# A decoder on one core: the recurrent cell's last steps and the head of causal attention, from generators and a scheduler to one written list of steps

## The chip, the cores and the metric

The program runs on one core of one Trainium2 chip. The metric is the device time of that core in microseconds (us), from the start of the program to its end. The core's engines have one instruction queue each and run beside one another: PE (TensorE: matrix products, and PEld for its weight loads), DVE (VectorE), ACT (ScalarE), POOL (GpSimd) and SP (SyncE, which issues DMAs). An engine works through its queue in order, and an instruction that waits for another engine holds everything behind it on its own.

## The reference, cut to what matters

The reference is a pre-norm decoder of two layers on `x` of 2 x 1024 x 256, all in float32. The change lies where the first layer's recurrent cell ends and the second layer's causal attention begins:

```python
def step(c, xt):
    ft = sigmoid(xt @ wf.T + c @ uf.T + bf)
    it = sigmoid(xt @ wi.T + c @ ui.T + bi)
    gt = tanh(xt @ wc.T + c @ uc.T + bc)
    return ft * c + it * gt, None
c_final, _ = lax.scan(step, c0, x)              # two steps: the leading axis of x is time
h = tanh(einsum('tbi,oi->tbo', x, wo) + c_final @ uo.T + bo)     # both steps' rows
...
qkv = einsum('bsd,hde->bhse', x, Wqkv) + bqkv   # 16 heads of 16, on the normed x
score = where(causal, einsum('bhsd,bhtd->bhst', q, k), -inf)
attn = softmax(score / sqrt(16)); y = attn @ v  ...  out = y @ Wout + bout
```

Both are residual: `x = x + cell(norm(x))`, then `x = x + causal(norm(x))`. Cross attention and a mixture of experts follow and end the program.

## The kernel before, in words

**The cell** (class `Cell`). Rows are held as 16 tiles of 128 rows; the normed x is held transposed (`xT[0]` for the first time step, `xT[1]` for the second). `gates(pool, step, state)` computes a step for two column halves `nb` and two halves `mc` of the features: three gates each, a gate being 2 (first step) or 4 (second step) float32 products of 128x128 by 128x512 into a PSUM tile `ps_t` (L1370), a sigmoid or tanh on ACT (L1378), and three DVE operations that make the new state (L1385 to L1388). `out(pool, t)` adds the cell's output to one of the 16 tiles of x: four products of 128x256 (L1411), a bias add on DVE (L1415), tanh on ACT (L1416), and the add to x on DVE (L1417).

**Causal attention** (class `Causal`). Eight units `u` = batch entry x group of four heads; each head takes 32 of the 128 partitions. `prepare(b)` clears the values (POOL), takes the norm's statistics (DVE, a power on POOL), norms (ACT, L1480), adds an output bias to x on POOL (L224), transposes (PE, L1489; copied by ACT, L1490) and makes the values (PE, L1496; DVE, L1503). `project(u)` makes four halves of keys and queries (PE, L1524; bias on ACT, L1531). `maxima(u)` takes the row maxima that the softmax subtracts, in 24 steps: for one query tile and a pair of heads (`pr` 0 or 1, so half of the 128 partitions) two products of 32 rows by up to 512 columns into one tile `ps_s` (L1565), on the diagonal a causal add on DVE (L1573), and a reduction on DVE (L1581). `augment(u, half)` transposes the maxima and adds them to the queries (L1591, L1593). `attend(u)` has 24 steps too: scores of a pair of heads into two tiles `ps_t` (L1640), exponentials on ACT (L1675), a mask on POOL (L1633), and, two entries late (`LAG`), the product with the values into `ps_o` (L1605).

**PSUM.** Under `banks("ps_e", 2, 4, 0)` there are two `ps_s` and four `ps_t` tiles, under `banks("ps_b", 2, 3, 1)` two, three and one `ps_o`.

**What sets the order.** `cell.scan` (both steps of the cell) is written in program order. The 16 `out` steps, `prepare(0)` and `project(0)` (generator `start`) stand outside a manual schedule, so the framework's scheduler orders them, with four `ps_t`. Then the cell's memory is closed, `Cross` is built (its weights are loaded by SP, L2699 on, and it clears and masks small tiles on POOL, L1857 to L1878), and `causal.run` follows in program order: twelve steps of maxima of unit 0 beside the eight projection halves of units 1 and 2, `augment(0, 0)`, then the loop over units. In the loop's pass for unit 0 each of the first eight steps runs two maxima and each of the other sixteen runs one, so that the maxima come to stand 20 steps ahead of the attention (`LEAD`):

```python
        for i in range(n - self.LEAD + 8):
            max_step()
            next(side, None)
        self.augment(0, 0)
        ...
                max_step()
                if u == 0 and i < 8:
                    max_step()
                next(attend, None)
```

From unit 1 on a step is one step of maxima and one of attention. Two earlier parts of the kernel are already played from lists of single steps by the function `play`.

Of the kernel before, what the change touches and what calls it, by code (L numbers as in the profile page):

```python
# [18 lines left out]
F32 = mybir.dt.float32  # L19
# [267 lines left out]
def play(order, *objects):  # L287

    for step in order.split():
        other = step.endswith("'")  # L290
        name, args = step.rstrip("'").rsplit("_", 1)
        to = objects[name.startswith("l_")]
        name = name.removeprefix("l_")
        getattr(to, "h0_" if name == "h0" else name)(*(int(a) for a in args), *((True,) if other else ()))
# [995 lines left out]
class Cell:  # L1290

    GATES = (("wf", "uf", "bf"), ("wi", "ui", "bi"), ("wc", "uc", "bc"))
# [61 lines left out]
    def gates(self, pool, step, state):  # L1356
# [3 lines left out]
        for nb in range(2):  # L1360
            cols = slice(nb * 512, (nb + 1) * 512)
            for mc in range(DC):
                gates = []
                for gi, (wn, un, bias) in enumerate(self.GATES):
                    o = k.t()
                    pairs = [(w[wn], self.xT[step][:, kc, cols], kc) for kc in range(DC)]
                    if step:
                        pairs += [(w[un], state[:, kc, cols], kc) for kc in range(DC)]
                    for n, (wm, rhs, kc) in enumerate(pairs):
                        nc.tensor.matmul(  # L1370
                            o,
                            lhsT=wm[:, kc, mc * P : (mc + 1) * P],
                            rhs=rhs,
                            start=(n == 0),
                            stop=(n == len(pairs) - 1),
                        )
                    gt = pool.tile([P, 512], F32, tag=f"gate{gi}", bufs=2, name=f"gate{gi}")
                    nc.scalar.activation(  # L1378
                        gt, o, AF.Tanh if gi == 2 else AF.Sigmoid,
                        bias=k.vec(bias, mc) if step else self.gb[:, gi, mc : mc + 1],  # L1380
# [5 lines left out]
                if step:  # L1386
                    nc.vector.tensor_mul(f, f, state[:, mc, cols])
                    nc.vector.tensor_add(new[:, mc, cols], f, i)  # L1388
                else:
                    nc.vector.scalar_tensor_tensor(  # L1390
                        new[:, mc, cols], f, k.vec("in_c", mc), i, ALU.mult, ALU.add
                    )

    def scan(self, pool):
# [4 lines left out]
        for n, _ in enumerate(self.gates(pool, 0, None)):  # L1399
            next(side, None)  # L1400
        drain(side)
        drain(self.gates(pool, 1, self.state))

    def out(self, pool, t):

        k, nc = self.k, self.k.nc
        rows = slice((t % TB) * P, (t % TB + 1) * P)
        lhs = [(self.xT[t // TB], "wo", c) for c in range(DC)] + [(self.state, "uo", c) for c in range(DC)]
        o = k.t()[:, :D]
        for n, (a, name, c) in enumerate(lhs):  # L1410
            nc.tensor.matmul(  # L1411
                o, lhsT=a[:, c, rows], rhs=self.w[name][:, c, :], start=(n == 0), stop=(n == len(lhs) - 1)
            )
        h = pool.tile([P, D], F32, tag="h", bufs=3, name="h")
        nc.vector.tensor_add(h, o, k.row("cell_bo"))  # L1415
        nc.scalar.activation(h, h, AF.Tanh)  # L1416
        nc.vector.tensor_add(self.x[:, t, :], self.x[:, t, :], h)  # L1417
# [5 lines left out]
class Causal:  # L1423
# [11 lines left out]
    LAG = 2  # L1435

    def __init__(self, k, x, wt, pool):
# [16 lines left out]
        self.xT, self.vr, self.q, self.kt, self.oS = {}, {}, {}, {}, {}  # L1454
        self.waiting = []

    def prepare(self, b):

        k, nc, pool, x = self.k, self.k.nc, self.pool, self.x
        xT = self.xT[b] = pool.tile([P, DC, N], F32, tag="xT", bufs=2, name="xT")  # L1460
        vr = self.vr[b] = pool.tile([P, TB, 16, 32], F32, tag="vr", bufs=2, name="vr")
        nc.gpsimd.memset(vr, 0.0)
        nc.gpsimd.memset(vr[:, :, :, AUG], 1.0)
        st, mv = k.small([P, TB, 6], "pr_st", 1), k.small([P, TB, 2], "pr_mv", 1)
        u = k.small([P, TB], "pr_u", 1)
        for i in range(TB):
            nc.vector.bn_stats(st[:, i, :], x[:, 8 * b + i, :])
            if i == 3:
                yield
        for i in range(TB):  # L1470
            nc.vector.bn_aggr(mv[:, i, :], st[:, i, :])
        nc.vector.tensor_scalar_add(u, mv[:, :, 1], EPS)
        r = k.rsqrt(u, TB)
        yield
        nc.vector.scalar_tensor_tensor(u, mv[:, :, 0], -1.0, r, ALU.mult, ALU.mult)
        for g in range(2):
            xh = pool.tile([P, 4, D], F32, tag="xh", bufs=1, name="xh")
            for i in range(4):
                j = 4 * g + i
                nc.scalar.activation(  # L1480
                    xh[:, i, :], x[:, 8 * b + j, :], AF.Identity, bias=u[:, j : j + 1], scale=r[:, j : j + 1]
                )
            k.add_row(x[:, 8 * b + 4 * g : 8 * b + 4 * g + 4, :], "bout")
            yield
            s = k.s()
            for kc in range(DC):
                for i in range(4):
                    at = (kc * 4 + i) * P
                    nc.tensor.transpose(s[:, at : at + P], xh[:, i, kc * P : (kc + 1) * P], k.ident)  # L1489
            nc.scalar.copy(xT[:, :, g * 512 : (g + 1) * 512], s.rearrange("p (c n) -> p c n", c=DC))  # L1490
            yield
        for t in range(0, TB, 4):
            s = k.s()
            for i in range(4):
                for kc in range(DC):
                    nc.tensor.matmul(  # L1496
                        s[:, i * D : (i + 1) * D],
# [1366 lines left out]
```

## Time and profile before

| what | value |
|---|---|
| median of four runs | 1698.52 us (1694.68 to 1700.31) |
| the profiled execution: its time, and the span in its trace | 1698.14 us, 1696.1 us |
| PE busy, DVE busy, ACT busy, POOL busy (share of the span) | 97%, 48%, 31%, 18% |
| mean granted clock of PE | 0.982 |
| second step of the cell | 591.3 to 632.5 us |
| outputs, preparation, projection of unit 0 | 632.5 to 679.1 us |
| twelve maxima beside the projections of units 1 and 2, first augment | 679.1 to 705.0 us |
| unit 0's pass of the loop, from its first scores | 707.5 to 760.0 us |
| units 1, 2 and 3 | from 760.0, 821.0 and 865.3 us on (61.0 us for unit 1, 44.3 us for unit 2) |

How to read it: times inside the trace count from the span's start; the execution's own time is 2.0 us more than its span. A row of busy time by stretch gives, for each engine, busy us and, in brackets, how many instructions; `PEclk` in it is the share of full speed that PE's clock was granted. A group's row gives the line, the engine, what is written from what, the number, the busy time and the mean of one. In the timeline a row has start, length, engine, line, and in square brackets how long the engine had been idle and who ended that. A matmul's shown length overlaps the next one's, so a step's price is taken from start to start. In float32 the trace shows two records for each matmul of the program.

### The profile page before, as it was taken

How to read it: one execution, taken by the hardware profiler on the slowest of the kernel's cores; microseconds unless marked ns; L12 is line 12 of the kernel's file. 1: busy time of each engine (PE TensorE's matmuls, PEld its weight loads, DVE VectorE, ACT ScalarE, POOL GpSimd, SP SyncE). 2: the span in 40 equal slices, each digit the busy share in tenths (PEclk: the TensorE clock that was granted, in tenths of full speed). 3: DMA queues.
4: the chain of work that ended last, by engine and by line, in shares of the span. 5: the costliest groups of instructions: out<-in, count | busy, mean ns of one | idle time of the engine just before them, and what ended most of it. 6: DMA issues, size and time to landing. Idle time of an engine off the chain costs nothing. (4 is left out here: it accounts for less than half of the span.)

```text
span 1696.1 us, 21340 instructions
## 1 busy us (share of the span) xinstructions
PE 1638.4 (97%) x8816; PEld 882.5 (52%) x8822; DVE 807.1 (48%) x1450; ACT 524.6 (31%) x890; POOL 300.9 (18%) x372
## 2 busy tenths in 40 slices
PE   7999999999999999899999999989999999999998
PEld 5756544443432547333434433546785665566466
DVE  8714555475544425676677668375721311111322
ACT  2321412333233223245455455443311111111110
POOL 2003301322123203013111011200054000000520
PEclk9999999999999999889999999998999999999999
DMA  6000000000000101000000000070033322232321
GB/s 236 0 1 3 0 0 1 1 1 1 1 1 0 41 1 33 0 2 1 1 2 1 1 1 2 27 252 2 1 136 100 124 91 96 62 124 73 108 64 50
DMA packets 36824, 69.68 MB, mean 41 GB/s; under 512 B 5048, under 2 KB 28152, under 8 KB 36344
## 3 DMA queue, kind: packets, MB, share of 16 engines
q1 hardware_dynamic: 28712, 53.61, 9.5%
q0 software_dynamic: 4608, 11.54, 2.2%
q10 hardware_dynamic: 3408, 3.17, 0.5%
q8 instruction: 70, 1.15, 0.3%
q14 instruction: 26, 0.21, 0.0%
HBM read 54.15 MB, written 14.16 MB: 40 GB/s over the span
## 5 line engine op out<-in xcount | busy, mean ns | idle before, releaser
L2591 PE MATMUL ps_s<-xe,w 128*128 128x512 f32 (+1 forms) x528 | 229.0, 592 | 0.0
L1675 ACT ACTIVATE pT<-ps_t 128x512 f32<-128x512 f32 (+3 forms) x344 | 150.6, 490 | 148.1 <-PE ps_t L1640 145.7
L1565 PE MATMUL ps_s<-kT,qT 32*128 32x512 f32 (+3 forms) x768 | 180.3, 561 | 10.9 <-DVE part L1581 7.0
L2606 DVE TENSOR_TENSOR hid<-ga,ps_s 128x512 f32<-128x512 f32 (+3 forms) x99 | 62.1, 628 | 267.0 <-ACT ga L2602 267.0
L1640 PE MATMUL ps_t<-qT,kT 32*128 32x512 f32 (+3 forms) x688 | 184.0, 553 | 2.2 <-ACT pT L1675 2.2
L2591 PEld LDWEIGHTS ps_s<-xe,w 128*128 128x128 f32 (+1 forms) x528 | 98.0, 187 | 121.3 <-issue 120.0
L2618 PE MATMUL ps_o<-wo,hid 128*128 128x256 f32 (+1 forms) x704 | 153.7, 379 | 0.0
L1581 DVE TENSOR_REDUCE part<-ps_s 128x2 f32<-128x1024 f32 (+3 forms) x128 | 130.5, 1024 | 46.1 <-PE ps_t L1640 38.8
L2618 PEld LDWEIGHTS ps_o<-wo,hid 128*128 128x128 f32 (+1 forms) x704 | 133.2, 190 | 18.5 <-issue 0.5
L2602 ACT ACTIVATE ga<-ps_s 128x512 f32<-128x512 f32 (+3 forms) x99 | 54.4, 549 | 249.1 <-PE ps_s L2591 249.0
L1633 POOL TENSOR_SCALAR_AFFINE_SELECT pT<-pT 128x256 f32<-128x256 f32 x128 | 52.2, 409 | 316.9 <-ACT pT L1675 309.4
L1085 DVE TENSOR_REDUCE part<-ps_s 128x2 f32<-128x1024 f32 x64 | 77.3, 1220 | 61.0 <-PE ps_s L1075 60.4
L1565 PEld LDWEIGHTS ps_s<-kT,qT 32*128 32x128 f32 x768 | 60.4, 192 | 87.6 <-issue 44.1
L1605 PE MATMUL ps_o<-pT,vr 128*32 128x256 f32 (+4 forms) x1408 | 99.4, 361 | 1.8 <-POOL pT L1633 1.5
L1209 ACT ACTIVATE pT<-ps_s 128x1024 f32<-128x1024 f32 x64 | 65.5, 1024 | 113.3 <-PE ps_s L1202 112.1
L1573 DVE TENSOR_TENSOR ps_s<-ps_s,causal 128x256 f32<-128x256 f32 x128 | 55.0, 430 | 65.6 <-PE ps_t L1640 44.6
L1214 POOL TENSOR_TENSOR acc<-acc,pT 128x1024 f32<-128x1024 f32 x24 | 56.4, 2350 | 162.8 <-ACT pT L1209 152.2
L2591 PE MATMUL ps_s<-xin,w 128*128 128x256 f32 (+3 forms) x264 | 79.0, 458 | 1.9 <-DVE xT L133 1.4
L1605 PEld LDWEIGHTS ps_o<-pT,vr 128*32 128x32 f32 x1408 | 29.0, 109 | 99.2 <-issue 85.3
L1640 PEld LDWEIGHTS ps_t<-qT,kT 32*128 32x128 f32 x688 | 70.4, 190 | 11.3 <-ACT pT L1675 7.1
L1075 PE MATMUL ps_s<-kT,qT 64*128 64x512 f32 x256 | 70.3, 634 | 0.8 <-DVE part L1066 0.8
L1129 PE MATMUL ps_o<-pT,vr 128*64 128x512 f32 x256 | 69.5, 624 | 0.9
(412 smaller groups left out, 2351.9 us busy)
## 6 DMA issues: line engine op xcount, KB each, us to landing
w<-in_w SPq DMA_DIRECT2D x32, 684.0 KB, 8.4
wo<-in_wo SPq DMA_DIRECT2D x8, 1280.0 KB, 6.9
xi_rows<-xin SPq DMA_DIRECT2D x8, 384.0 KB, 8.7
eo_rows<-rows ACTq DMA_DIRECT2D x12, 256.0 KB, 4.9
xr<-xi_rows POOLq DMA_DIRECT2D x48, 64.0 KB, 7.2
w_ffn<-in_w_ffn SPq DMA_DIRECT2D x1, 2304.0 KB, 14.2
x<-in_x SPq DMA_DIRECT2D x4, 512.0 KB, 5.4
w<-in_w_cell SPq DMA_DIRECT2D x2, 1024.0 KB, 17.1
```

The lines of the kernel that those rows point to most:

```text
L1075: self.k.nc.tensor.matmul(s3[:, hh, :], lhsT=self.q[u][rows, qt * P : (qt + 1) * P], rhs=self.kt[u][rows, half * 512 : (half + 1) * 512], ...
L1085: self.k.nc.vector.tensor_reduce(self.part_of(u)[:, half, qt, :], s3, AX.X, ALU.max, negate=True)
L1129: nc.tensor.matmul(self.o[hh * 64 : hh * 64 + 64, :], lhsT=self.vr[b][:, kk, h * 64 : (h + 1) * 64], rhs=pT[:, hh, :], start=first, stop=last,
L1209: nc.scalar.activation(pT, s3, AF.Exp)
L1565: nc.tensor.matmul(s3[:, hh, :n], lhsT=q[rows, qt * P : (qt + 1) * P], rhs=kt[rows, at : at + n], start=True, stop=True,)
L1581: nc.vector.tensor_reduce(out, s3[:, :, :n], AX.X, ALU.max, negate=True)
L1605: nc.tensor.matmul(self.o[hh * 32 : hh * 32 + 32, cols], lhsT=vr[:, kk, 4 * grp + hh, :], rhs=pts[hh // 2][:, hh % 2, cols], start=first, ...
L1640: nc.tensor.matmul(out, lhsT=kt[rows, kk * P : (kk + 1) * P], rhs=q[rows, j * 512 + q0 : (j + 1) * 512], start=True, stop=True,)
L1675: nc.scalar.activation(pT[:, hh, q0:], heads[hh][:, q0:], AF.Exp)
L2591: self.k.nc.tensor.matmul(s[:m, i * 512 : i * 512 + n], lhsT=wt[:, kc, at : at + m], rhs=self.inputs[e][:, kc, first : first + n], start=( ...
L2606: self.k.nc.vector.tensor_mul(self.hid[:m, hc, first : first + n], self.act.pop(hc)[:m, :n], self.now.pop(hc)[:m, 512 : 512 + n])
L2618: self.k.nc.tensor.matmul(o, lhsT=self.hid[:n, hc, st * P : (st + 1) * P], rhs=self.to[:n, hc, :], start=(hc == 0), stop=(hc == len(HCH) - 1),
```

## The change

The cell's second step, its 16 outputs, the preparation of batch entry 0, the projections of units 0, 1 and 2, all 24 maxima of unit 0, the first eight of unit 1 and both augments of unit 0 become single steps, which `play` runs in the order of one written list, `TURN_ORDER`, under the banks `ps_b` (three `ps_t` where these stages had four). A name in the list is a step, its digits (base 36) its arguments, `l_` the `Causal` object, and a quote mark moves a PSUM copy from ACT to DVE: `gate` is one gate's products, `act` its activation, `comb` the state; `prod`, `hadd`, `tanh`, `xadd` are one output tile; `zero` to `vadd` are the preparation; `proj` and `pcopy` a half of keys or queries; `max` is the two products of one step of maxima and `red` its DVE part; `aug` and `qaug` the augment. The preparation is now done in two groups of four tiles, with a power of four columns for each (`root`) in place of one of eight. The loop's pass for unit 0 is left with twelve maxima (8 to 19 of unit 1), one at every second step. The first step of the cell and the units from 1 on are arranged as before. The cell's memory stays open to the list's end, so `Cross` is built, and its weights are loaded, after the list. Matrix products, reductions and DMAs are the same in number; six PSUM copies go from ACT to DVE.

```diff
         name = name.removeprefix("l_")
-        getattr(to, "h0_" if name == "h0" else name)(*(int(a) for a in args), *((True,) if other else ()))
+        getattr(to, "h0_" if name == "h0" else name)(*(int(a, 36) for a in args), *((True,) if other else ()))
...
-        drain(self.gates(pool, 1, self.state))
+        self.pool, self.old, self.of = pool, self.state, {}
+        self.state = pool.tile([P, DC, N], F32, tag="state", bufs=2, name="state")
...
+    def gate(self, nb, mc, gi):
+        nc, cols = self.k.nc, slice(nb * 512, (nb + 1) * 512)
+        wn, un, _ = self.GATES[gi]
+        o = self.of["g", nb, mc, gi] = self.k.t()
+        pairs = [(wn, self.xT[1], kc) for kc in range(DC)] + [(un, self.old, kc) for kc in range(DC)]
+        for n, (name, of, kc) in enumerate(pairs):
+            nc.tensor.matmul(
+                o, lhsT=self.w[name][:, kc, mc * P : (mc + 1) * P], rhs=of[:, kc, cols],
+                start=(n == 0), stop=(n == len(pairs) - 1),
+            )
+
+    def act(self, nb, mc, gi):
+        k = self.k
+        gt = self.pool.tile([P, 512], F32, tag=f"gate{gi}", bufs=2, name=f"gate{gi}")
+        k.nc.scalar.activation(
+            gt, self.of["g", nb, mc, gi], AF.Tanh if gi == 2 else AF.Sigmoid, bias=k.vec(self.GATES[gi][2], mc)
+        )
+        self.of["g", nb, mc, gi] = gt
+
+    def comb(self, nb, mc):
+        nc, cols = self.k.nc, slice(nb * 512, (nb + 1) * 512)
+        f, i, g = (self.of["g", nb, mc, gi] for gi in range(3))
+        nc.vector.tensor_mul(i, i, g)
+        nc.vector.tensor_mul(f, f, self.old[:, mc, cols])
+        nc.vector.tensor_add(self.state[:, mc, cols], f, i)
...
+    def prod(self, t):
...
+    def hadd(self, t):
+        self.k.nc.vector.tensor_add(self.of["h", t], self.of["o", t], self.k.row("cell_bo"))
+
+    def tanh(self, t):
+        self.k.nc.scalar.activation(self.of["h", t], self.of["h", t], AF.Tanh)
+
+    def xadd(self, t):
+        self.k.nc.vector.tensor_add(self.x[:, t, :], self.x[:, t, :], self.of["h", t])
+
...
+TURN_ORDER = """
+gate_000 l_zero_0 gate_002 act_000 gate_112 act_002 gate_001 act_112 gate_010 act_001 comb_00 gate_012
+act_010 gate_011 act_012 gate_111 act_011 comb_01 prod_1 act_111 prod_3 hadd_1 tanh_1 xadd_1 prod_0 hadd_3
+tanh_3 xadd_3 prod_2 hadd_0 tanh_0 xadd_0 gate_100 hadd_2 tanh_2 xadd_2 l_stat_00 l_mean_00 gate_110
+act_100 l_root_00 l_shift_00 l_norm_00 gate_101 act_110 l_bias_00 comb_11 l_turn_00 act_101 gate_102
+l_xcopy_00' l_proj_110 act_102 comb_10 l_proj_100 l_pcopy_110' prod_6 l_pcopy_100 l_max_11 hadd_6 prod_5
+tanh_6 l_red_11 xadd_6 l_max_10 hadd_5 prod_4 tanh_5 l_red_10 xadd_5 l_max_14 hadd_4 tanh_4 l_max_13
+xadd_4 l_proj_000 l_red_13 l_red_14 prod_7 l_pcopy_000' l_max_12 hadd_7 prod_e l_red_12 tanh_7 xadd_7
+l_stat_01 l_max_17 l_val_00 l_mean_01 l_red_17 l_root_01 l_shift_01 hadd_e l_norm_01 l_max_15 l_vadd_00
+prod_c l_red_15 tanh_e l_bias_01 l_turn_01 hadd_c xadd_e l_xcopy_01 l_max_16 l_proj_010 l_red_16 tanh_c
+xadd_c l_proj_011 l_pcopy_010 l_max_03 l_pcopy_011' l_max_01 l_red_03 l_proj_201 l_red_01 l_max_0c
+l_pcopy_201 l_max_04 l_red_0c l_proj_101 l_red_04 l_max_05 l_pcopy_101 l_max_0e l_red_05 l_proj_211
+l_red_0e l_max_0k l_pcopy_211' l_max_07 l_red_0k l_proj_001 l_red_07 l_max_0d l_pcopy_001 l_max_09
+l_red_0d prod_d l_red_09 l_max_0b l_red_0b l_max_0a prod_9 hadd_d l_red_0a tanh_d l_max_0n xadd_d l_max_0i
+l_red_0n l_proj_200 l_red_0i l_max_0m hadd_9 l_max_0j l_red_0m tanh_9 prod_a l_red_0j l_max_0f hadd_a
+l_pcopy_200' tanh_a l_max_00 l_red_0f prod_8 l_red_00 l_max_0g xadd_9 l_val_01 l_red_0g xadd_a hadd_8
+tanh_8 xadd_8 l_max_02 l_vadd_01 prod_f l_red_02 l_max_06 hadd_f tanh_f l_max_0h l_red_06 prod_b l_red_0h
+xadd_f l_aug_00 l_qaug_00 l_max_08 l_proj_111 hadd_b l_red_08 tanh_b l_max_0l xadd_b l_pcopy_111
+l_proj_210 l_red_0l l_part_0 l_aug_01 l_pcopy_210 l_qaug_01
+"""
...
+    def zero(self, b):
+        nc = self.k.nc
+        vr = self.vr[b] = self.pool.tile([P, TB, 16, 32], F32, tag="vr", bufs=2, name="vr")
         nc.gpsimd.memset(vr, 0.0)
         nc.gpsimd.memset(vr[:, :, :, AUG], 1.0)
-        st, mv = k.small([P, TB, 6], "pr_st", 1), k.small([P, TB, 2], "pr_mv", 1)
-        u = k.small([P, TB], "pr_u", 1)
-        for i in range(TB):
-            nc.vector.bn_stats(st[:, i, :], x[:, 8 * b + i, :])
-            if i == 3:
-                yield
-        for i in range(TB):
-            nc.vector.bn_aggr(mv[:, i, :], st[:, i, :])
-        nc.vector.tensor_scalar_add(u, mv[:, :, 1], EPS)
-        r = k.rsqrt(u, TB)
...
+    def root(self, b, g):
+        self.of["r", b, g] = self.k.rsqrt(self.of["v", b, g], 4)
...
+    def norm(self, b, g, vector=False):
...
+    def bias(self, b, g):
+        self.k.add_row(self.group(b, g), "bout")
...
+    def xcopy(self, b, g, vector=False):
+        out = self.xT[b][:, :, g * 512 : (g + 1) * 512]
+        in_ = self.of["t", b, g].rearrange("p (c n) -> p c n", c=DC)
+        if vector:
+            self.k.nc.vector.tensor_copy(out, in_)
+        else:
+            self.k.nc.scalar.copy(out, in_)
...
+    def pcopy(self, u, w, nb, vector=False):
+        k, grp = self.k, u % 4
+        out, s = (self.kt, self.q)[w][u][:, nb * 512 : (nb + 1) * 512], self.of["p", u, w, nb]
+        bias, scale = ((k.vec("sk_b", grp), 1.0), (self.qb[:, grp : grp + 1], 0.25))[w]
+        if vector:
+            k.nc.vector.tensor_scalar(out, s, scale, bias, ALU.mult, ALU.add)
+        else:
+            k.nc.scalar.activation(out, s, AF.Identity, bias=bias, scale=scale)
...
+    def max(self, u, i):
+        qt, half, pr, n = self.a[i]
+        s3 = self.of["m", u, i] = self.k.s().rearrange("p (h n) -> p h n", h=2)
+        for hh in range(2):
+            rows = slice((2 * pr + hh) * 32, (2 * pr + hh) * 32 + 32)
+            self.k.nc.tensor.matmul(
+                s3[:, hh, :n],
+                lhsT=self.q[u][rows, qt * P : (qt + 1) * P],
+                rhs=self.kt[u][rows, half * 512 : half * 512 + n],
+                start=True,
+                stop=True,
+            )
...
+    def red(self, u, i):
+        nc, (qt, half, pr, n) = self.k.nc, self.a[i]
+        s3 = self.of.pop(("m", u, i))
+        if half * 512 + n == (qt + 1) * P:
+            nc.vector.tensor_tensor(
+                s3[:, :, n - P : n],
+                s3[:, :, n - P : n],
+                self.k.causal.unsqueeze(1).to_broadcast([P, 2, P]),
+                ALU.add,
...
+        nc.vector.tensor_reduce(out, s3[:, :, :n], AX.X, ALU.max, negate=True)
...
-        ahead = iter(())
-        made = 0
+        made = n + self.DONE
+        ahead = self.maxima(1, self.DONE)
...
-        side = chain(self.project(1), self.project(2))
-        for i in range(n - self.LEAD + 8):
-            max_step()
-            next(side, None)
-        self.augment(0, 0)
+        side = iter(())
...
-                max_step()
-                if u == 0 and i < 8:
+                if u or i % 2 == 0:
                     max_step()
...
-                if i == (4 if last else n - self.LEAD + 2):
+                if u and i == (4 if last else n - self.LEAD + 2):
...
-        with k.banks("ps_e", 2, 4, 0), tc.tile_pool(name="cell", bufs=1, reuse_waits="tile") as pool:
+        pool = cell_pool.enter_context(tc.tile_pool(name="cell", bufs=1, reuse_waits="tile"))
+        with k.banks("ps_e", 2, 4, 0), tc.manual_schedule():
+            cell.scan(pool)
+        with k.banks("ps_b", 2, 3, 1):
             with tc.manual_schedule():
-                cell.scan(pool)
-            for t in range(TB):
-                cell.out(pool, t)
-
-            for t, _ in zip_longest(range(TB, NT), causal.start()):
-                if t is not None:
-                    cell.out(pool, t)
-        cell_pool.close()
-        cross = Cross(k, x, weights("w_cross", N_CROSS), a["ctxT"], const)
-        with k.banks("ps_b", 2, 3, 1), tc.tile_pool(name="self_b", bufs=1, reuse_waits="tile") as late:
-            with tc.manual_schedule():
+                play(TURN_ORDER, cell, causal)
+            cell_pool.close()
+            cross = Cross(k, x, weights("w_cross", N_CROSS), a["ctxT"], const)
+            with tc.tile_pool(name="self_b", bufs=1, reuse_waits="tile") as late, tc.manual_schedule():
                 causal.run(late, cross.stats())
     with tc.tile_pool(name="moe", bufs=1, side="right") as mp:
 
```

## The prediction

> **What bounds the kernel now.** I read the page first: the list of engines, then the row of clocks.
>
> ```profile
> PE 1638.4 (97%) x8816; PEld 882.5 (52%) x8822; DVE 807.1 (48%) x1450; ACT 524.6 (31%) x890; POOL 300.9 (18%) x372
> ...
> PEclk9999999999999999889999999998999999999999
> ```
>
> PE is busy almost always; what can be won is its idle time and the time at a lowered clock. The two eights are the slices from 678 to 763 us, which is where the change works. Next, busy time by stretch there (length, then busy us and number for PE, PEld, DVE, ACT, POOL, then the clock):
>
> ```profile
> 591.30:679.10 87.80, 85.39 (x291) 53.15 (x289) 31.68 (x66) 24.21 (x43) 13.41 (x21) 1.00 0.06 16
> 679.10:705.00 25.90, 23.52 (x84) 9.19 (x85) 13.87 (x25) 6.78 (x9) 0.00 (x0) 1.00 0.00 0
> 705.00:707.50 2.50, 2.48 (x9) 1.26 (x11) 1.04 (x2) 0.00 (x0) 0.00 (x0) 0.53 0.03 7
> 707.50:760.00 52.50, 48.68 (x373) 20.10 (x369) 39.15 (x53) 20.68 (x48) 6.54 (x16) 0.83 0.00 1
> ```
>
> From the second step of the cell to 679 PE works at full clock with 2.4 us of idle time; little is to be had. Unit 0's pass (last row) takes 52.5 us at clock 0.83, with DVE busy 39.2 us. Unit 2, which has no such start, takes 44.3 us (821.0 to 865.3) with 7.7 us of projections in it. So the loss sits in unit 0's pass. The same view, asked for the stretches ahead of three falls of the clock and for the one behind the first:
>
> ```profile
> 701.70:705.10 3.40, 1.69 (x14) 1.19 (x15) 3.29 (x8) 0.70 (x1) 0.00 (x0) 1.00 0.00 0
> 715.40:718.80 3.40, 2.29 (x14) 0.64 (x12) 3.24 (x5) 0.99 (x3) 0.82 (x2) 1.00 0.00 0
> 725.70:729.10 3.40, 1.81 (x16) 1.09 (x12) 3.26 (x7) 0.66 (x2) 0.41 (x1) 0.99 0.00 0
> 705.20:712.00 6.80, 6.80 (x26) 3.19 (x27) 4.30 (x5) 1.09 (x2) 0.41 (x1) 0.50 0.01 2
> ```
>
> Each time DVE is full (3.2 to 3.3 of 3.4 us), PE waits for it and is busy for 1.7 to 2.3 us, and then PE has half its clock for 6.8 us. The waits view names the pair:
>
> ```profile
> PE ps_s L1565 <- DVE part L1581: 5.2, 8, 1.3
> ```
>
> Maxima wait for the reduction that frees one of two `ps_s`. Lastly the price of a maximum, in PE's timeline: alone between projections, and in a later step beside scores.
>
> ```profile
> 688.84 1.13 PE L1565 MATMUL ps_s<-kT,qT 32*128 32x512 f32 x4
> 689.90 1.98 PE L1524 MATMUL ps_t<-xT,w 128*128 128x512 f32 x4
> 691.82 1.13 PE L1565 MATMUL ps_s<-kT,qT 32*128 32x512 f32 x4
> ...
> 754.80 0.70 PE L1565 MATMUL ps_s<-kT,qT 32*128 32x512 f32 x2
> 754.81 0.70 PE L1640 MATMUL ps_t<-qT,kT 32*128 32x512 f32 x2
> 755.33 0.59 PE L1565 MATMUL ps_s<-kT,qT 32*128 32x512 f32 x2
> 755.34 0.59 PE L1640 MATMUL ps_t<-qT,kT 32*128 32x512 f32 x2
> 755.87 0.64 PE L1605 MATMUL ps_o<-pT,vr 128*32 128x256 f32 x8
> ```
>
> From start to start a maximum of 512 columns alone costs 1.06 us; a maximum and scores, on opposite halves of the partitions, together cost 1.07 (754.80 to 755.87). Beside scores it is free.
>
> **The change part by part.** Counted from the second step's first product, at 591.3 us, to unit 1's first scores: 168.7 us before (to 760.0).
>
> *The list on PE.* Twelve gates at 3.43 (593.00 to 596.43 in the timeline) are 41.2; 16 outputs at 1.73 are 27.7; two transposes 1.8; two value products at 3.45, 6.9; twelve projection halves at 1.72, 20.6; two augments 0.9. That is 99.1, unchanged in work. The maxima: 32, of which unit 0's twelve of 512, four each of 384, 256 and 128 columns, and unit 1's first eight, two of each width. The rows of 679 to 700 give 1.06, 0.85, 0.63 and 0.43 alone, and the projection behind one takes 1.92 in place of 1.72 (689.90 to 691.82). In each price some 0.2 is the change between the two kinds of product, since 512 columns twice at a projection's pace are 0.86. Columns alone then sum to 19.8. In the list the 32 stand in 21 runs: eleven times two maxima stand with no other product between, and eight of these pairs use opposite heads, which can overlap by up to 4.3. So 19.8 + 21 x 0.4 = 28.2 without overlap, 23.9 with all of it. The list is 123.0 to 127.3 if PE never waits.
>
> *Does it wait?* On DVE the stretch from `max_03` to `red_00` is the densest: reductions at 1.2, 0.95, 0.66, 0.4 for the four widths, 0.45 for each causal add, 0.7 for each copy, 0.36 for each add make 26 us against PE's 30.8 before overlap. DVE is nearly full there, but PE has projections and outputs to put between, which unit 0's pass did not have. I followed the list with a maximum handed over in 0.1 us (PE to DVE) and 0.15 us (back), as in the rows at 679 to 703: second maxima of a pair wait some tenths, no step longer than one. Elsewhere the covers hold: the norm of group 0 (statistics 1.4, aggregate 0.45, power 1.0, ACT 2.1) lies under three gates (10.3), that of group 1 under a value product, a maximum and an output (6.2). POOL's two bias adds (2.36 each) hold up adds on DVE, as at 655 us (1.88 for an add of 0.42); the second comes among maxima, with two projections behind it as cover. The six copies moved to DVE are in its 26 and in the norm's cover. Three `ps_t` for four cost nothing while a copy comes within two products (3.4 us). I take 124.5: waits bring back part of the overlap.
>
> *After the list.* ACT copies the last query half, loads its table (1.28) and starts exponentials some 0.5 us after the first scores: +0.5. `Cross`'s setup on POOL (7.5 us, at 671 to 679 before) and its seven DMAs now follow the last `prod`; POOL's first mask queues behind it. `prod_b` ends 6 us ahead of the list's end, so POOL is free about 2 us into the pass, near the first mask: 0, at worst 2. Those weights are read only after the last unit has begun.
>
> *Unit 0's pass.* It keeps 24 scores, its products and twelve maxima. Unit 2 without its four projections (4 x 1.92) and one augment (0.5) is 44.3 - 8.2 = 36.1; half as many maxima saves nothing there, for a paired one is free, and scores go at 1.75 us a step (749.45 to 759.98 holds six) because the third `ps_t` waits for ACT. I add 2.0 for one fall of the clock at its start, where the first steps have no product behind the scores. From 0 to 7 is possible: before, three falls lay in the pass.
>
> Sum: 124.5 + 0.5 + 36.1 + 2.0 = 163.1, against 168.7: 5.6 us less. The profiled execution took 1698.1 (span plus 2.0), so 1692.5; the median, 1698.5, is 0.4 above it. Later units are as before and PE-bound, so nothing gives the gain back; the second power of four columns in `prepare` (1.0 for two, where one of eight took 1.64) is off the path.
>
> [...] The falls here come after gaps of at most 1.3 us (702.4), summing to 1.1 to 1.7. [...]
>
> **The rivals.**
>
> *The gain is eaten, no change (1697).* Two or three falls in unit 0's pass as before (each 6.8 us at half clock costs up to 3.4) or one in the list. For it: with two of four row groups busy and no products, the pass starts thin. Against: DVE's 39 us there shrink to about 15. Price: 4 us back.
>
> *Slower (1706).* The clock falls in the list's second half. From `max_11` on PE has 71 us of work, more than a third of it maxima, and DVE is filled to four fifths; if PE waits for DVE as in 705 to 736 (20.4 of 30.7 us at half clock), five falls cost up to 3.4 each, 17; as DVE catches up meanwhile I count 13.5, which leaves it 8 slower. It decides by number: the second fall uses up the gain, the fourth makes it measurably slower. Against: 679 to 701 mixes maxima and projections at clock 1.00.
>
> *The list does not fill PE (1695 to 1700).* If hand-overs cost 0.2 us more at each of 32, the 6.4 cancel the gain. The change then does not do what its form promises.
>
> **How the numbers follow.** About 0.3% (5.1 us: 1693.4 and 1703.6) is what a measurement of this kernel can tell from no change. Forecast, a gain of 2.5 to 12 (list 122 to 126, pass 34 to 40): 0.62, most of it beyond 5.1 us. Gain eaten or list not filled: 0.23. Slower: 0.15. Faster by over 0.3%: 0.50; within: 0.36; slower: 0.14. The range leaves out a tenth on each side: from 1685 (all overlap, no fall) to 1702.
>
> **What would show it.** Right: PE without idle time above 1 us and at clock 1.00 from 591 to about 716; unit 0's first scores near 717, unit 1's near 754; one fall at most between; DVE some 15 us busy in the pass. Wrong: waits of maxima for reductions above 6 us in the list; falls inside it; a first mask waiting for `Cross`'s setup; unit 1 starting after 759.

## The result, and the profile after

The changed kernel takes 1698.5 us (median of 44 runs, 1687.3 to 1710.3) against 1697.25 us for the kernel before on the same chip (70 runs): a ratio of 1.0016, 95% interval 1.0006 to 1.0027. That is within 0.3%, on the slow side; a gain of 0.33% had been forecast. The profiled execution took 1703.2 us, 4.7 above the median, with a span of 1701.3 and a mean clock of 0.982. The ratios of the experiments below leave out five runs at a lower clock: one of the control, three with maxima on the same heads, and one of 2742.1 us with early fillers.

The page of the changed kernel first, the engines' line and the row of clocks in 40 slices:

```profile
PE 1649.0 (97%) x8816; PEld 883.2 (52%) x8822; DVE 812.0 (48%) x1460; ACT 520.2 (31%) x884; POOL 302.3 (18%) x374
...
PEclk9999999999999999979999999998999999999999
```

Where two slices stood at eight, from 678 to 763 us, one now stands at seven (from 723 to 766). PE is busy 10.6 us more than before with the same number of instructions. The clock over the whole program does not explain that: its mean is 0.982 in both executions. It fits the maxima: of the 32 that unit 0's pass held, 20 now stand in the list, where no scores run beside them, and PE's busy time up to the pass goes from 111.4 us (591.3 to 707.5 before) to 125.1. Next, busy time by stretch of the changed kernel, the list, unit 0's pass and unit 1 (length, then busy us and number for PE, PEld, DVE, ACT, POOL, then the granted clock, DMA share, GB/s).

```profile
592.55:717.80 125.25, 125.09 (x457) 67.39 (x455) 73.54 (x132) 24.99 (x45) 12.77 (x20) 1.00 0.04 12
717.80:764.60 46.80, 45.57 (x293) 17.52 (x292) 15.86 (x20) 22.48 (x51) 7.66 (x19) 0.74 0.01 1
764.60:827.80 63.20, 58.54 (x444) 25.89 (x440) 35.69 (x64) 30.86 (x65) 16.68 (x22) 0.89 0.00 1
```

The list is what was forecast: 125.3 us (124.5 in the sum), PE idle for 0.16 us of it, clock 1.00 throughout. The pass is not: DVE is down to 15.9 us as expected, PE is almost always busy, and yet it takes 46.8 us where 0.5 + 36.1 + 2.0 = 38.6 were expected. The clock, 0.74, is lower than in the pass before (0.83). The same view, cut at the edges of the one fall of the clock:

```profile
717.10:720.50 3.40, 2.63 (x20) 1.43 (x20) 1.76 (x3) 3.00 (x5) 1.81 (x4) 1.00 0.08 23
720.50:723.90 3.40, 3.40 (x22) 1.95 (x16) 1.55 (x3) 2.94 (x8) 1.31 (x4) 1.00 0.00 0
723.90:747.80 23.90, 23.44 (x123) 8.29 (x124) 4.96 (x7) 7.71 (x21) 3.98 (x10) 0.50 0.00 1
747.80:764.60 16.80, 16.80 (x142) 6.35 (x139) 7.58 (x8) 9.17 (x21) 1.22 (x3) 1.00 0.01 2
```

In the 3.4 us ahead of the fall PE is busy for all 3.40, and it then has half its clock for 23.9 us, in which it is again busy for 23.44. Before, three falls of 6.8 us each came after stretches in which PE had waited for DVE. Here PE waits for nothing in the stretch ahead of the fall, and the fall is longer than those three together. PE's waits from 715 to 765 are a single line, the longer of the two (0.77 us) just ahead of that stretch:

```profile
PE ps_t L1774 <- ACT pT L1809: 1.2, 2, 0.8
```

A second thing stands in PE's timeline. The prediction let a maximum beside scores be free, because the two use opposite halves of the partitions. In the new pass, half of the maxima belong to the heads whose scores come next. Some of these start beside the scores of the step before; three have a product in between and stand alone. One that overlaps, and one that does not:

```profile
749.45 0.70 PE L1678 MATMUL ps_s<-kT,qT 32*128 32x512 f32 x2
749.46 0.71 PE L1774 MATMUL ps_t<-qT,kT 32*128 32x512 f32 x2
...
752.88 1.13 PE L1678 MATMUL ps_s<-kT,qT 32*128 32x512 f32 x4
753.85 1.02 PE L1774 MATMUL ps_t<-qT,kT 32*128 32x512 f32 x4
```

So there were two suspects, pairing and clock, and for the clock several causes.

### The profile page after: what moved, and what is told of

It reads as the page before. It is cut to its first block, busy times and chain, and to the rows that moved or that the text cites. A ratio compares the mean times of both kernels' runs of the same rounds, so it can differ in the third digit from the quotient of the medians.

```text
span 1701.3 us, 21347 instructions
## 1 busy us (share of the span) xinstructions
PE 1649.0 (97%) x8816; PEld 883.2 (52%) x8822; DVE 812.0 (48%) x1460; ACT 520.2 (31%) x884; POOL 302.3 (18%) x374
## 5 line engine op out<-in xcount | busy, mean ns | idle before, releaser
L1700 DVE TENSOR_REDUCE part<-ps_s 128x2 f32<-128x1024 f32 (+3 forms) x128 | 130.9, 1024 | 65.0 <-PE ps_t L1774 45.8
L1678 PEld LDWEIGHTS ps_s<-kT,qT 32*128 32x128 f32 x768 | 59.5, 189 | 75.1 <-issue 42.9
```

Source lines behind the costliest of these rows:

```text
L1678: self.k.nc.tensor.matmul(s3[:, hh, :n], lhsT=self.q[u][rows, qt * P : (qt + 1) * P], rhs=self.kt[u][rows, half * 512 : half * 512 + n], s ...
L1700: nc.vector.tensor_reduce(out, s3[:, :, :n], AX.X, ALU.max, negate=True)
```

## Experiments

**Theory 1** (pairing): maxima placed ahead of scores of their own heads cost the lost time. **Theory 2**, later **R**: the clock falls because few of PE's 128 rows are in use (a head's products use one group of 32 of them), although PE is busy. **Theory 3**: the wait of 0.77 us for the exponential's table (its load on ACT took 1.28 us, from 718.18 on) at the pass's start sets off the fall. Rivals inside theory 2 are the array's area in place of its rows (**A**) and the mean load of the whole pass.

"Pass" is from unit 0's first scores to unit 1's, in each kernel's own trace; "half" is the time in it at half clock. The ratio is to the kernel before on the same chip. The three sets of experiments ran on other chips than the result; there the kernel before takes 1720.9, 1722.8 and 1722.6 us, most of the difference after the causal units: from the last unit's first scores to the end the traced runs need 668 to 678 us in place of 644. In every kernel that keeps the full list, it took 125.3 us (125.6 in one, with two copies moved).

| kernel | list | pass | half | ratio (95%) |
|---|---|---|---|---|
| before | | 52.5 | 18.1 | |
| changed | 125.3 | 46.8 | 23.9 | 1.0016 (1.0006 to 1.0027) |
| changed, control | 125.3 | 46.8 | 23.9 | 0.9995 (0.9969 to 1.002) |
| opposite heads | 125.3 | 45.3 | 23.9 | 0.9987 (0.9961 to 1.0014) |
| same heads | 125.3 | 64.4 | 56.3 | 1.0063 (1.0031 to 1.0095) |
| filled | 125.3 | 36.6 | 0 | 0.9988 (0.997 to 1.0006) |
| twenty in the pass | 118.4 | 39.6 | 3.4 | 0.9958 (0.9939 to 0.9977) |
| filled, narrow | 125.3 | 42.9 | 0 | 1.0009 (0.999 to 1.0029) |
| two projections late | 121.5 | 41.6 | 0 (6.8 in the list) | 0.9966 (0.9943 to 0.9988) |
| table early | 125.6 | 40.7 | 10.2 | 0.9974 (0.9945 to 1.0004) |
| filled early | 125.3 | 36.0 | 0 | 0.9956 (0.9931 to 0.9981) |
| filled late | 125.3 | 40.5 | 10.2 | 1.0004 (0.9982 to 1.0027) |
| filled, own parity | 125.3 | 37.7 | 0 | 0.9972 (0.9947 to 0.9997) |
| one projection late | 118.7 | 42.7 | 6.8 | 0.9933 (0.9913 to 0.9954) |

The whole time carries falls from everywhere in the kernel: unit 1 alone has 3.4 to 13.6 us at half clock and takes 58.7 to 63.2 us in these traces, with the same work. So the pass in the trace decides between theories, and the ratio says what is left of it.

### Opposite heads, and its mirror

Two kernels, one with each of the added lines:

```diff
-                if u or i % 2 == 0:
+                if u or i % 4 in (0, 3):        # opposite heads
+                if u or i % 4 in (1, 2):        # same heads
                     max_step()
```

> The changed kernel with one line altered: in unit 0's pass the twelve maxima go ahead of steps 0, 3, 4, 7, 8 and so on instead of every even step, so that each stands beside scores of the other head pair. The order list is untouched. In the changed kernel's trace three of the twelve (starting at 736.14, 752.88 and 760.34 us) stood alone, 2.0, 1.0 and 1.0 us, ahead of scores of their own heads. Theory 1 (pairing): these 4.0 us go, and some of the smaller ones; unit 0's pass goes from 46.8 to 42 to 43 us, and the time to about 0.9992 of the kernel before (from 1.0016). Theory 2 (the clock falls because two of four row groups are idle): maxima are as many as before, so the fall of 23.9 us stays within some us; theory 2 alone gives a pass of 46 to 47. Theory 3 (the 0.77 us start wait for the exponential's table sets off the fall): as theory 2, the fall stays.

> The mirror of the run before: the twelve maxima of unit 0's pass go ahead of steps 1, 2, 5, 6, 9, 10 and so on, where every one stands ahead of scores of its own head pair. Theory 1: where a product of the probabilities lies between, each costs its 1.0 us alone (2.0 at half clock): three such in the changed kernel become eight to twelve, so the pass goes from 46.8 to 50 to 54 us and the time to 1.004 to 1.006 of the kernel before. A theory in which only the clock counts: pass about 47, ratio about 1.0016.

With every maximum beside opposite heads the pass is 45.3 us: 1.5 less, not 4 to 5, and the fall has the same 23.9 us. Theory 1 is real but small. With all on the same heads the pass is 64.4 us, beyond what theory 1 gave (50 to 54): two falls of 27.3 and 30.7 us cover 56.3 of it (the second ends 1.8 us after the pass). Placing alone, with the same products, more than doubled the time at half clock. Against the run with opposite heads that is 32.4 us more at half clock, worth up to 16.2 of the 19.1 us by which the pass is longer; the price of lone maxima is left with some 3.

### Filled steps

```diff
+    def idle(self, u, i):
+        kk, pr, q0 = self.b[i][1:]
+        s3 = self.k.s().rearrange("p (h n) -> p h n", h=2)
+        for hh in range(2):
+            rows = slice((2 - 2 * pr + hh) * 32, (2 - 2 * pr + hh) * 32 + 32)
+            self.k.nc.tensor.matmul(s3[:, hh, : 512 - q0], lhsT=self.q[u][rows, :P],
+                rhs=self.kt[u][rows, q0:512], start=True, stop=True)
...
                 if u or i % 4 in (0, 3):
                     max_step()
+                else:
+                    self.idle(0, i)
```

> As the run with opposite heads, and at the twelve steps of unit 0's pass that have no maximum a product of the same kind is added on the other head pair (its result is read by nobody, so the output is unchanged): PE gets 24 more small products and all four row groups are in use in every step. Theory 2 (array use sets the clock): the fall shrinks to at most 7 us or goes, and the pass is 37 to 40 us, 3 to 5 less than in the run with opposite heads alone, although work was added; ratio 0.996 to 0.997. Theory 3 (start wait) or a clock that falls at random: the fall stays, the pass is as in the run with opposite heads or up to 3 us longer.

Twelve steps of useless work made the pass 8.7 us shorter (45.3 to 36.6), because the fall is gone. Busy time of the filled kernel over the same first two stretches of 3.4 us, and the rest:

```profile
715.50:718.90 3.40, 3.08 (x21) 1.48 (x22) 1.76 (x3) 2.97 (x5) 1.85 (x4) 1.00 0.13 27
718.90:722.30 3.40, 3.40 (x26) 2.40 (x23) 1.32 (x3) 2.95 (x8) 1.22 (x3) 1.00 0.02 5
722.30:752.80 30.50, 29.32 (x302) 11.97 (x300) 11.56 (x14) 16.83 (x41) 5.30 (x13) 1.00 0.00 1
```

Second row against the changed kernel's second row: PE is busy for 3.40 us in both. In one kernel the clock halves right after it, in the other it stays whole. Busy time does not tell them apart; the rows in use do (1459 against 1901, counted as below). In these traces the clock changes on a grid of 3.413 us (see the section on counting), whose position does not separate the two: in the changed kernel's trace and in this one an edge of it lies 0.8 us ahead of the pass's first scores. The whole kernel is at 0.9988, where 0.996 to 0.997 was expected, with an interval that takes in no change: unit 1 had 13.6 us at half clock in this trace, 6.8 in the run with opposite heads, which is 3.4 us back.

### Twenty maxima in the pass

The list loses unit 1's eight `l_max_1x` and `l_red_1x`; the pass takes twenty, one for each of its first twenty steps, all opposite.

```diff
-    DONE = 8
+    DONE = 0
...
-                if u or i % 2 == 0:
+                if u or i < 20:
```

> Unit 1's first eight maxima leave the list; unit 0's pass takes twenty, one ahead of each of steps 0 to 19, all on the head pair opposite to the step's scores. The computation is complete. Eight maxima alone are 5.9 us by the rows of one (twice 1.06, 0.85, 0.63, 0.43), so the list goes from 125.3 to about 119. Theory 1: the pass has eight more maxima and still gets shorter, 42 to 43 us with the fall, since each is free beside opposite scores; together about 161 against 172.1, ratio about 0.995. Theories 1 and 2: all row groups are in use from the first step, no long fall, pass 38 to 39, ratio about 0.993. If maxima are not free even when opposite (0.9 us each): the pass is 50 or more and the ratio stays at 1.001 or above.

List 118.4, pass 39.6 with a single fall of 3.4 us: eight more maxima in a pass that got 7.2 us shorter. Together 158.0 us against 172.1 in the changed kernel, and 0.9958 of the kernel before. The pass is near the 38 to 39 that theories 1 and 2 together gave, and outside the 42 to 43 of theory 1 alone; the ratio is nearer to the 0.995 of theory 1 alone than to their 0.993.

### Counting the array's use

What does the clock follow? The starts of all falls of a trace lie whole multiples of 3.413 us apart (a grid, which each trace has in another place; in the traces of before and changed, with 12 and 8 falls, the fitted step is 3.4133 us and no start is off by more than 0.003), so I cut each trace on that grid and summed, for every product of PE, the rows in use / 128 times the moving columns. Products with the values (128 rows by 32 columns of weights) start in fours (at 748.11 in the changed kernel four start within 0.02 us, the next four 0.19 us after them; eight with 256 columns take 0.57 us from start to start, where as many columns of a projection take 1.72), and I count each as a quarter. A projection does 4 x 512 in 1.72 us, so a full stretch is 2048 x 3.413 / 1.72, some 4060. The eight score records at 720.66 in the changed kernel (32 rows, 512 columns) are 8 x 512 x 32 / 128 = 1024 in 2 us.

| stretch of 3.4 us that the fall follows, from | count |
|---|---|
| before, 701.7, 715.4 and 725.6 us | 800, 1425, 726 |
| changed, 720.5 (PE busy 3.40) | 1459 |
| opposite heads, 714.0 | 1312 |
| same heads, 716.1 and 746.8 | 1102, 1456 |
| twenty in the pass, 710.4 | 1452 |
| no fall: filled, from 715.5 and 718.9 | 2481, 1901 |

Of several counts tried on the first six traces (busy time, columns alone, area), area fitted best: rows times columns of weights in use, which is the same number in the rows above. The next kernels test it. The count by rows, as given here, was set on the ten traces at hand after them, ahead of the last four kernels.

### Narrow fillers, an early table, two projections late

The control is the changed kernel unaltered:

> The changed kernel again, as a control beside the next three. Every theory expects list 125.3 us and unit 0's pass 44 to 47, with a long stretch at half clock in the pass, and 1.000 to 1.003 of the kernel before.

It repeated the pass to the tenth: 46.8 us, 23.9 at half clock. Then the fillers with 32 columns of weights:

```diff
-                s3[:, hh, : 512 - q0], lhsT=self.q[u][rows, :P],
+                s3[:32, hh, : 512 - q0], lhsT=self.q[u][rows, :32],
```

> The run with filled steps, but the added products use 32 columns of weights in place of 128 (their result is again read by nobody): as many instructions, as many moving columns, the same four row groups, a quarter of the array's area. Counted over the six traces so far, a fall of the clock follows a stretch of 3.4 us in which rows times columns in use, over 128 x 128, times moving columns sum to less than about 1480 (at full use it would be some 4060). Theory A (area): the added products count 32 to 64 per step in place of 128 to 256, the first stretches stay under 1480, the fall stays at 17 us or more and the pass is 44 to 47. Theory R (row groups, or simply PE's occupation): all four row groups are in use as in the filled run, so no fall of more than 7 us, pass 36 to 40.

No fall: theory A is wrong, R right about the clock. The pass's first whole stretch, from 715.8, counts 985 by area and 1601 by rows. The pass was still 42.9, longer than R gave. PE's timeline shows why: in the narrow kernel (first two rows) a filler did not run beside the scores, as against the filled one.

```profile
742.18 1.05 PE L1691 MATMUL ps_s<-kT,qT 32*32 32x512 f32 x4 [0.31 <-DVE part L1713]
743.15 1.13 PE L1787 MATMUL ps_t<-qT,kT 32*128 32x512 f32 x4
```

```profile
740.86 0.70 PE L1691 MATMUL ps_s<-kT,qT 32*128 32x512 f32 x2 [0.30 <-DVE part L1713]
740.88 0.70 PE L1787 MATMUL ps_t<-qT,kT 32*128 32x512 f32 x2
```

One after the other took 0.97 + 1.06 from start to start, beside one another 1.07. The pass is 6.3 us longer than the filled one, 0.5 for each of the twelve.

In the kernel with an early table, `l_pcopy_111` and `l_pcopy_210` get the quote mark (VectorE):

> The changed kernel with the last two copies of the list on VectorE in place of ScalarE, so that ScalarE loads the exponential's table some 1 us earlier. Theory 3 (the start wait of 0.77 us sets off the fall): the wait goes, no long fall, pass 46.8 to 37 to 39, ratio 0.996. Theory A: without that wait PE still has only scores and maxima there, the long fall stays (20 us or more) and the pass is 45 to 47, ratio 1.000 to 1.002.

The wait shrank to 0.27 us, and a fall still began 4.7 us into the pass, after a stretch that counts 1396. So theory 3, by which the wait of 0.77 us sets it off, does not hold. But the fall lasted 10.2 us, not 20, and the pass was 40.7: shorter than the 45 to 47 of theory A too. By the count, the stretch from 727.5 reached 1544 and ended it. This is one trace, on one position of the grid; how much the wait adds to the length is not settled.

Last of this set, the kernel with twenty maxima in the pass, with `l_proj_200`, `l_proj_210` and their copies taken from the list:

```diff
                 next(attend, None)
+                if u == 0 and i in (1, 4):
+                    self.proj(2, i == 1, 0)
+                    self.pcopy(2, i == 1, 0, True)
```

> The run with twenty maxima in the pass, and two of unit 2's four projections leave the list and stand after steps 1 and 4 of unit 0's pass (copied by VectorE). The computation is complete. Each is 2048 full-array columns, 1.72 us. List 118.4 to 114.6 to 115. Theory A: the 3.4 us fall 5 us into the pass goes, since its stretch stood at 1453 and gains up to 2048; pass 39.6 - 1.7 + 3.4 = 41.3; list and pass together 156 against 158.0; ratio to the kernel before 0.993 to 0.996. A clock that falls at random, or because of the start wait: the fall stays as often, pass 43, together 158, no gain.

The fall at the pass's start is gone and the pass is 41.6, as expected. The list is not: 121.5 in place of 114.6 to 115, and the ratio, 0.9966, misses 0.993 to 0.996. PE's waits in list and pass of this kernel:

```profile
PE ps_s L1676 <- DVE part L1698: 2.2, 3, 1.2
PE ps_s L1717 <- DVE mneg L1702: 1.6, 1, 1.6
```

PE now waits for reductions, one stretch of the list, from 680.3, counts 945, and the clock falls for 6.8 us inside the list. The projections had been the cover of those waits.

### Where the fillers stand

```diff
-                else:
+                elif i < 8:                  # filled early
+                elif i >= 8:                 # filled late
                     self.idle(0, i)
```

> The run with opposite heads, and added products (unread, as in the filled run, 128 columns of weights) at steps 1, 2, 5 and 6 alone: 4 of the 12. Theory R, now as a count over ten traces: the clock falls after a stretch of 3.4 us in which rows in use over 128, times moving columns (products on different column groups beside one another counted once), sum to under 1490, of some 4060 at full use; it returns only after a stretch of over 1510. Once the clock is halved, scores alone cannot give that, so one thin stretch at the start holds the clock down for 24 us. By it the first stretch goes from 1312 to 1600 or more, later stretches of the run with opposite heads stand at 1606 to 2515 when the clock is whole, so: no fall of more than 7 us in the pass, pass 34 to 38. A theory in which the mean load of the pass counts: a third of the fillers, a fall of some 14 to 18 us, pass 41 to 44.

> The same, with the added products at the eight later steps alone (9, 10, 13, 14, 17, 18, 21, 22). Theory R: the first stretches are as thin as in the run with opposite heads, so the clock falls within 7 us of the pass's start and stays down until the fillers come, 10 to 24 us; pass 41 to 46. Mean load: two thirds of the fillers, fall under 10 us, pass 37 to 41.

Four fillers at the start do what twelve did (36.0 us, no fall), where mean load gave a fall of 14 to 18 us and a pass of 41 to 44. With the eight later ones alone the fall comes. It then lasts 10.2 us, and the pass, 40.5, lies in the range of mean load (37 to 41), just below that of R (41 to 46). But the fillers did not shorten it, for the first of them starts after its end, at 729.01:

```profile
729.57 0.70 PE L1691 MATMUL ps_s<-kT,qT 32*128 32x512 f32 x2
```

Up to there this kernel runs the same products as the one with opposite heads, whose fall lasted 23.9 us. The two traces differ in where the grid lies: its first edge in the pass comes 1.4 us after the first scores here and 0.5 us there. So over the same products the fall lasted 10.2 and 23.9 us, in two traces that differ in where the grid lies, and this run says nothing of how fillers end one. Filled early first, then filled late, cut at the same places:

```profile
716.50:719.90 3.40, 3.08 (x22) 2.01 (x20) 0.63 (x2) 3.04 (x6) 0.82 (x2) 1.00 0.00 0
719.90:723.30 3.40, 3.11 (x33) 1.63 (x29) 1.58 (x4) 2.01 (x6) 1.22 (x3) 1.00 0.02 5
723.30:750.80 27.50, 26.74 (x246) 10.50 (x246) 10.89 (x12) 15.74 (x37) 4.49 (x11) 1.00 0.00 1
```

```profile
715.30:718.80 3.50, 2.73 (x14) 1.86 (x15) 0.73 (x2) 3.21 (x7) 0.82 (x2) 1.00 0.00 0
718.80:729.00 10.20, 9.73 (x59) 3.66 (x55) 2.63 (x6) 3.28 (x10) 2.45 (x6) 0.50 0.01 2
729.00:754.40 25.40, 24.57 (x248) 9.74 (x244) 10.01 (x10) 14.59 (x32) 3.27 (x8) 1.00 0.01 1
```

The counts of the first rows are 1791 and 1115. In the second kernel the fall ends with the stretch from 725.6, which counts 1609 at half clock; inside the long falls of the changed kernel and of the run with opposite heads they count 905 to 1519, but for the last of each.

> The changed kernel with its own placing of the twelve maxima (ahead of even steps, half of them of the step's own heads), and added unread products of the opposite heads at the odd steps. With the clock held up by the fillers this prices the pairing by itself. Theory R: no fall of more than 7 us. Theory 1 (pairing): three to six maxima stand alone at 1.0 us, so the pass is 36.6 + 3 to 6 = 39.6 to 42.6. If pairing costs little (as 46.8 against 45.3 suggests): 36.6 to 38.

With the clock held up, the changed kernel's own placing costs 37.7 - 36.6 = 1.1 us. The grid lies here within 0.1 us of where it lies in the changed kernel's trace. That is the size of theory 1, below the 3 to 6 us it had been given.

### One projection late

From the kernel with twenty maxima: `l_proj_210` and its copy leave the list, `l_pcopy_111` gets the quote mark.

```diff
                 next(attend, None)
+                if u == 0 and i == 1:
+                    self.proj(2, 1, 0)
+                    self.pcopy(2, 1, 0, True)
```

> The run with twenty maxima in the pass, with one projection of unit 2 (the last of the list) moved behind step 1 of the pass, and the last copy of the list on VectorE. The computation is complete. The list keeps the other projections, whose removal left PE idle (a stretch of 945, then a fall of 6.8 us) when two were moved. List 118.4 - 1.7 = 116.7 without a fall; pass 39.6 - 1.7 + 1.7 = 39.6, with no fall at its start since its thin stretch (1452) gains up to 2048; together 156.3 against 158.0 for the run it is made from and 168.7 for the kernel before; ratio to the kernel before 0.992 to 0.996. If the fall stays: 158, ratio 0.995 to 0.997.

The ratio is as expected, 0.9933 (0.9913 to 0.9954), but the stages are not: list 118.7, pass 42.7, together 161.4 against 158.0. PE's longest wait in list and pass is one that the kernel with twenty maxima did not have:

```profile
PE ps_s L1717 <- DVE mneg L1702: 2.0, 1, 2.0
```

and the clock around it, from the last stretch of the list on:

```profile
706.60:710.00 3.40, 1.70 (x15) 1.02 (x18) 2.55 (x5) 0.00 (x0) 2.93 (x6) 1.00 0.33 85
710.00:716.90 6.90, 6.90 (x18) 2.21 (x17) 2.24 (x5) 2.28 (x4) 0.81 (x2) 0.51 0.00 1
```

The augment now waits 2.0 us for the maxima of the second half, which the moved projection had covered. That makes the first row's stretch thin (1376), and the clock falls for 6.8 us. The intervals of this kernel and of the one it was made from (0.9939 to 0.9977) overlap, so the runs do not say which is faster. Both beat the kernel before. Beside the changed kernel's control (0.9969 to 1.002, in another set), this one's interval lies clear of it, and that of the kernel with twenty maxima overlaps it by 0.0008.

## Why the prediction was wrong

- **The list: right.** 125.3 us for 124.5; no wait of PE, no fall. The rival "the list does not fill PE" and the one of falls in its second half did not come.
- **DVE, mask, table: right.** DVE is busy 15.9 us in the pass (some 15). The first mask did not wait for `Cross`. The table's wait is 0.77 us for the 0.5 given.
- **Unit 0's pass, 36.1 us: right in itself.** With the clock whole it is 36.6 (filled) and 36.0 (filled early).
- **"A paired one is free": wrong in part.** It assumed opposite heads for all twelve. The placing costs 1.1 to 1.5 us.
- **"I add 2.0 for one fall of the clock": this is the step that failed.** With its own placing and the clock held up, the pass is 37.7; as it is, 46.8. The fall costs 9.1 us where the sum had 2.0 and allowed 7 at most. 36.6 + 1.1 + 9.1 = 46.8, and unit 1 starts at 764.6, past the 759 that the prediction had set as a sign against it.

The reason stands in the reading of the three falls before. I saw that each followed a stretch in which PE waited for DVE, and took the waits for the cause. The waits were one way to a thin stretch. Scores alone, on two of four row groups, are another, without any wait; and the maxima beside them were what had filled the other two. The change took twenty of the pass's 32 maxima away, and with them that fill (with twenty put back, the pass had one fall of 3.4 us). Once the clock is halved, a stretch holds about half as much (a maximum alone took 1.87 us from start to start at 736.14, at half clock, and 0.97 at 752.88): scores with few products then count 905 to 1519, while the clock returned only after stretches above 1500. That is why one fall could last 23.9 us, as it did in both traces of the changed kernel, where each fall before had lasted 6.8. In the run filled late, which up to its first filler has the products of the run with opposite heads (23.9 us), the fall lasted 10.2, with the grid in another place.

The rival "the gain is eaten" had the place ("with two of four row groups busy and no products, the pass starts thin") and the end (1697), by two or three short falls in place of one long one, so that its time came out is luck. Its counterargument, that DVE's 39 us shrink to about 15, held (15.9) and did not bear on the clock. In profiled executions, list, pass and unit 1 together went from 229.7 to 235.3 us; the medians differ by 1.25 us. The time at half clock differs from run to run, and the mean clock goes with the time: of the changed kernel's runs, one of 1687.4 us has 0.992, one of 1710.2 us 0.975. That a pass without the long fall is behind the fastest runs is not shown: they have no trace.

## What to carry to other kernels

Before products are moved from one stage to another, ask what they did for PE's clock where they stood: sum rows in use times columns for the stage that is left (here the clock fell after stretches of 3.413 us under 1500 of 4060), not PE's busy time. This pass started thin, and a few products on idle row groups at its very start kept the clock up (four steps of them, 36.0 us), while more of them later came too late (eight, 40.5 us); real work served too (twenty maxima in the pass, 39.6 us with a fall of 3.4). And a projection that seems to be in the way at the end of a list may be the cover of a wait: in both kernels that moved one, PE waited anew (1.6 and 2.0 us for the augment).

## What the runs showed of the hardware

- **PE's clock followed rows in use, on a grid.** In 14 traces, their first 40 us and last 15 us left out, 106 falls to half clock: 103 followed a stretch of the 3.413 us grid that counts under 1500 of 4060 (37%). The other three counted 1574, 1936 and 1943. Of 6409 stretches at full clock that no fall followed, three counted under 1500, the lowest 1489. The bound was set on ten traces; in the four after it, 27 of 29 falls lay under 1490, and no stretch under it was without a fall. No return to full clock came after a stretch of under 1500; some above (21) brought none. With the best single bound for each, the count by rows misplaces 3 of these stretches, area 27, busy time 62, columns alone 63. The counts rest on modelled starts and ends of the products; by how a product across an edge is split, single ones shift by up to 15.
- **Products of 32 x 32 did not run beside products of 32 x 128** on other rows: 2.03 us for the two from 742.18 in the narrow kernel, where two of 32 x 128 took 1.07 (740.86 in the filled one).
- **Added work shortened a stage**: with 24 useless products of the program the pass took 8.7 us less (36.6 for 45.3).
